# All additions of the experts' outputs on VectorE, and the last choice's outputs loaded over two queues

## The chip, the cores and the metric

The kernel runs on one core of one Trainium2 chip. The metric is the device time of one execution in microseconds (us). A kernel is run several times and the median counts; this kernel before the change has a median of 569.73 us over 3 runs (569.17 to 570.04).

## What is computed

One decoder layer on 1024 tokens of width 256 (16 sequences of 64). It has three parts: self-attention with block-scaled weights, cross-attention with rotary positions, and a mixture of experts. Only the last part matters here:

```
scores = softmax(xt @ Wg.T)                      # 16 experts in 4 groups
topi   = the best 4 experts of the best 2 groups
combine[t, topi] = scores[t, topi]
h = silu(einsum('td,eid->eti', xt, W1)) * einsum('td,eid->eti', xt, W3)
expert_out = einsum('eti,edi->etd', h, W2)
y = einsum('etd,te->td', expert_out, combine)
z = silu(xt @ Ws1.T) * (xt @ Ws3.T) @ Ws2.T      # shared expert
out = x + y + z                                  # x: the residual
```

So each token adds the outputs of four chosen experts ("choices"), each scaled by its score, to the residual.

## The kernel before

The residual `x` is held on chip as eight tiles `x[0]` to `x[7]` of 128 tokens x 256. Experts 0 to 14 are routed: rows of tokens are gathered, sorted by expert, from a buffer `xd` in device memory, an expert works on 384 slots at a time, and its output rows `y` are scattered to a buffer `yd` by three indirect DMAs that GpSimd issues (`send_outputs`, L1296). Expert 15 is the "dense" one: it works on all tokens (`dense_hidden`, `dense_output`), and its result is added to `x` straight from the accumulators, scaled by the token's weight (`add_last`, L944).

In the region of `yd` for choice k lie, for each token, the rows of its k-th choice in the order of the experts. The choices are sorted, so that choice 0 is complete when expert 11 has sent its rows, choice 1 after expert 12, choice 2 after expert 13 and choice 3 after expert 14. `load_outputs(k)` (L1306) then loads the four pieces of choice k, 256 KB each, into tiles `got`; its DMAs are issued by SyncE (L1312), and `behind(got, returned)` makes each of them wait for every scatter sent so far. There are 9 `got` buffers for the 16 pieces, so the later pieces take buffers that earlier additions have read.

`add_outputs(k, got, cw)` (L1319) adds choice k to the eight tiles. For i = 0, 1, 3, 4, 6, 7 VectorE does it in one instruction, `x[i] = y * w + x[i]` (L1326). For i = 2 and 5, ScalarE scales the piece in place (L1323) and GpSimd adds it (L1324). Additions to one tile follow each other in the order of the code.

The last part of the code puts choice 0's additions, the dense expert's output for the first half of the second 512 tokens, choice 1's additions, the dense expert's hidden layer and output for the rest, and choices 2 and 3. The dense expert's hidden layer is a chain over engines: matmuls, SiLU on ScalarE (`g`, L1275 and L1278), the product `h` on VectorE (L1276 and L1279), a rounded copy `hp` on ScalarE (L112), the remainder `hp` on VectorE (L113), and then the matmuls of the output. At the end eight DMAs store `x` (L1384), in turn from SyncE and ScalarE.

The code's order is not the order on an engine. The kernel is built with `schedule_with_timeline_sim=True`: at build time the framework runs the program on a timeline of its own and gives each engine the instruction that is ready there, earlier code first. `tc.issue_after(ins)` adds that an instruction stands behind `ins` on its engine. Once built, each engine works strictly through its list, so a wait holds up what stands behind it, DMA issues on that engine included.

The raw weights of each routed expert are loaded into one of two buffers `w123` of 128 x 1280 (L277) and split into two parts there by ScalarE (L278), VectorE and GpSimd (L283).

Of the kernel before, what the change touches and what calls it, by code (L numbers as in the profile page):

```python
# [25 lines left out]
F32 = mybir.dt.float32  # L26
# [3 lines left out]
AF = mybir.ActivationFunctionType  # L30
ALU = mybir.AluOpType
AX = mybir.AxisListType

B, S, D = 16, 64, 256
NT = B * S
NI = NT // 128
# [6 lines left out]
E, INTER, NGRP, TOPK, TOPKG = 16, 176, 4, 4, 2  # L43
# [4 lines left out]
W_COLS = W_UP + 2 * D  # L48
# [23 lines left out]
def decoder_layer(ctx: ExitStack, tc: tile.TileContext, a: dict, out: bass.AP):  # L72
    nc = tc.nc
# [17 lines left out]
    def av_tile():  # L91
        return ps_av.tile([128, 512], F32, tag="av", name="av")
# [24 lines left out]
    x = [t[:, i, :] for t in x_pairs for i in range(2)]  # L117
# [131 lines left out]
    def behind(read, writes):  # L249
        for w in writes:  # L250
            tc.add_manual_dep(
                read,
                w.name,
                mybir.DependencyInfo(mybir.DependencyClass.Sync, mybir.DependencyReason.DATA),
                reason="it reads rows of each",
            )
# [42 lines left out]
    def expert_output(ps, w, h_p, cols):  # L299


        w2 = [[p[:, W_UP + k * D : W_UP + (k + 1) * D] for p in w] for k in range(2)]
        h = [p[:, cols] for p in h_p]
        return matmuls(
            ps,
            [
                (h[0], w2[0][0]),
                (h[0], w2[0][1]),
                (h[1], w2[0][0]),
                (h[2], w2[1][0]),  # L310
                (h[2], w2[1][1]),
            ],
        )

    with ExitStack() as attn:
# [635 lines left out]
        with (  # L951
# [109 lines left out]
            def dense_weights():  # L1061

                parts = [
                    xw.tile([128, 2, 2, 4 * HQ], F32R, tag=f"w_q{n}", name=f"w_last{n}")
                    .rearrange("p a b c -> p (a b c)")[:, :W_COLS]
                    for n in range(2)
                ]
                up = xb.tile([128, 3, 2, 2, DC], F32, tag="w_s", name="w_last_up")
                down = xb.tile([128, 2, D], F32, tag="w_o0", name="w_last_down")
                for t, cols in (  # L1070
                    (up.rearrange("p a b c d -> p (a b c d)"), slice(0, W_UP)),
                    (down.rearrange("p a b -> p (a b)"), slice(W_UP, W_COLS)),
                ):
                    nc.sync.dma_start(out=t, in_=a["W123"][E - 1][:, cols])
                    parts_of(t, parts[0][:, cols], parts[1][:, cols])
                return parts
# [18 lines left out]
            def dense_gated(g, up, g2, up2):  # L1095
                h_p = [
                    xa.tile([128, 512], F32R, tag=f"roped1{n}", name=f"dense1{n}", bufs=1)
                    for n in range(2)
                ]
                h_p.append(xa.tile([128, 512], F32R, tag="q_r", name="dense2"))  # L1100
                nc.vector.tensor_tensor(g, up, g, ALU.mult)
                parts_of(g, h_p[0], h_p[1])
                nc.vector.tensor_tensor(g2[:64], up2[64:], g2[64:], ALU.mult)
                parts_of(g2[:64], h_p[2][:64], h_p[2][64:])
                return h_p
# [15 lines left out]
            for n in range(len(units) + 2):  # L1121
# [58 lines left out]
                if n == 8:  # L1180
                    w_last = dense_weights()
                    with after(exps[-1]):
                        routed.append(weights_of_choices(0))
                if n == 9:
# [30 lines left out]
                    with after(aimed, placed):  # L1215
# [4 lines left out]
                        h_p = dense_gated(*dense_ups)  # L1220
# [4 lines left out]
    fw = ctx.enter_context(tc.tile_pool(name="fw", bufs=2, reuse_waits="tile"))  # L1225
    fx = ctx.enter_context(tc.tile_pool(name="fx", bufs=2, reuse_waits="tile"))
    fh = ctx.enter_context(tc.tile_pool(name="fh", bufs=2, reuse_waits="tile"))
    fy = ctx.enter_context(tc.tile_pool(name="fy", bufs=2, reuse_waits="tile"))
# [3 lines left out]
    def expert_weights(src, down_lo=nc.gpsimd):  # L1232
        return weight_parts(
            src,
            fw.tile([128, W_COLS], F32, tag="w123", name="w123"),
            [
                fw.tile([128, W_COLS], F32R, tag=f"w123{n}", name=f"w123{n}", bufs=3)
                for n in range(2)
            ],
            down_lo,  # L1240
        )
# [63 lines left out]

    def load_outputs(k):  # L1306

        tiles = []
        for n in range(NI // 2):
            t = fy.tile([128, 2, D], F32, tag="got", name="got", bufs=9)  # L1310
            first = (E - 1) * SLOTS + (TOPK - 1 - k) * NT + n * 256
            got = nc.sync.dma_start(  # L1312
                out=t, in_=yd[first : first + 256].rearrange("(p i) d -> p i d", p=128)
            ).ins
            behind(got, returned)
            tiles.append(t)
        return tiles

    def add_outputs(k, got, cw):  # L1319
        for i in range(NI):  # L1320
            y, w = got[i // 2][:, i % 2], cw[i // 4][:, k, i % 4 : i % 4 + 1]
            if i % 3 == 2:
                nc.scalar.activation(y, y, AF.Copy, scale=w)  # L1323
                nc.gpsimd.tensor_tensor(x[i], x[i], y, ALU.add)  # L1324
            else:
                nc.vector.scalar_tensor_tensor(x[i], y, w, x[i], ALU.mult, ALU.add)  # L1326

    def dense_hidden(w, half, n):
        return expert_hidden(w, [p[:, :, n * 256 : n * 256 + 256] for p in normed[half]], 256)

    def dense_output(w, h_p, half, n, add):
        for b in range(2):
            ps = av_tile()[:, :D]
            expert_output(ps, w, h_p, slice(b * 128, b * 128 + 128))
            add(half, 2 * n + b, ps)
# [6 lines left out]
    ws, xs, hs, got = {}, {}, {}, {}  # L1342
    with tc.issue_after(lows[-1]), tc.issue_after(silus[-1]):
        ws[0] = expert_weights(a["W123"][0], nc.vector)
    for e in range(E + 1):
        if e in (1, 2):

            low = lows[-1]
            hs[e - 1] = expert_hidden(ws[e - 1], xs[e - 1][0], SLOTS)
        if e < E - 1:  # L1350
            low = lows[-1]
            with tc.issue_after(up_done[0] if e in (1, 2) else low):
                xs[e] = expert_inputs(e)
            if e >= 1:
                with tc.issue_after(low), tc.issue_after(silus[-1]):
                    ws[e] = expert_weights(a["W123"][e], nc.vector if e < 3 else nc.gpsimd)
        if e == 1:
            with tc.issue_after(gated[0]), tc.issue_after(silus[-1]):
                routed.append(weights_of_choices(1))
        if 0 <= e - 1 < E - 1 and e > 2:  # L1360
            hs[e - 1] = expert_hidden(ws[e - 1], xs[e - 1][0], SLOTS)
        if e - 2 >= 0:
            if e == E:

                with tc.issue_after(gated[0]):
                    h_p = dense_hidden(w_last, 1, 0)
            last = send_outputs(e - 2, ws.pop(e - 2), hs.pop(e - 2), xs.pop(e - 2)[1])
            if e - 2 == E - TOPK - 2:
                short = slots_are_short()
            k = e - 2 - (E - 1 - TOPK)  # L1370
            if k >= 0:
                got[k] = load_outputs(k)
    with ExitStack() as behind_last:
        for ins in (*last, gated[0]):
            behind_last.enter_context(tc.issue_after(ins))
        cw = [r[0] for r in routed]
        add_outputs(0, got[0], cw)
        dense_output(w_last, h_p, 1, 0, add_last)
        add_outputs(1, got[1], cw)
        dense_output(w_last, dense_hidden(w_last, 1, 1), 1, 1, add_last)  # L1380
        for k in range(2, TOPK):
            add_outputs(k, got[k], cw)
    for i in range(NI):
        (nc.sync if i % 2 == 0 else nc.scalar).dma_start(  # L1384
# [10 lines left out]
    with tc.If(short > 0):  # L1395
        w_over = [weights_without_slot(half, routed[half][2]) for half in range(2)]
        with tc.For_i(0, E - 1, 1) as e:
            w = expert_weights(a["W123"][bass.ds(e, 1)].rearrange("o p c -> p (o c)"))
            for half in range(2):
                dense_expert(w, half, add_over)  # L1400

                t = fs.tile([128, 4, E], F32, tag="slot", name="w_next")
# [110 lines left out]
```

## Time and profile before

| | |
|---|---|
| median of 3 runs | 569.73 us |
| the profiled execution | 570.74 us |
| its span, first to last instruction | 569.0 us |
| TensorE matmul busy | 537.4 us (94%) |
| VectorE busy | 400.9 us (70%) |
| ScalarE busy | 279.3 us (49%) |
| GpSimd busy | 230.5 us (41%) |
| last matmul starts | 559.66 us |
| last VectorE addition starts | about 564.0 us |

In the profile PE is TensorE, DVE is VectorE, ACT is ScalarE, POOL is GpSimd and SP is SyncE; a "q" behind a name marks work of the engine's sequencer, such as the issue of a DMA. Times are us from the start of the span. Instructions of one line that follow each other are merged in the timeline, with their number after an x; what stands in square brackets is the engine's idle time before them and what ended it. Matmuls fill the span up to about 546 us. The change lies wholly behind that, in the last 23 us.

### The profile page before, as it was taken

The page shows a single profiled execution, that of the slowest core. Times are in us where ns is not written, and L with a number is a line of the kernel's source. Part 1 is how long each engine was busy: PE and PEld are TensorE (multiplying, and loading weights), DVE is VectorE, ACT ScalarE, POOL GpSimd, SP SyncE. Part 2 cuts the span into 40 slices and gives each one's busy share as a digit, 9 for nine tenths or more (in the row PEclk, how much of TensorE's full clock was granted, in tenths as well). Part 3 has the DMA queues.
Part 4 walks back from the last instruction along what each step waited for, and adds up shares of the span by engine and source line. Part 5 has one row for each costly group of instructions (what it writes and reads, how often), then busy time and mean ns, then how long its engine had stood idle before and what let it go on. Part 6 is the DMA issues. An engine that isn't in the chain of part 4 may idle for free.

```text
span 569.0 us, 10603 instructions
## 1 busy us (share of the span) xinstructions
PE 537.4 (94%) x4013; PEld 444.5 (78%) x4013; DVE 400.9 (70%) x879; ACT 279.3 (49%) x524; POOL 230.5 (41%) x213
## 2 busy tenths in 40 slices
PE   7999999999999998999999999999999879999961
PEld 6888898988989876667687676676788779999961
DVE  5456555644555788767485686888878678999876
ACT  4677556575565533131323324143445368777551
POOL 4160500102000104434441445453445738888862
PEclk9999999999999999999999999999999989999995
DMA  8654431724300499564010000000322667776374
GB/s 213 163 170 129 129 106 44 205 95 108 97 1 1 119 289 277 140 188 127 2 52 20 8 1 1 0 30 1 105 106 80 209 217 255 244 249 239 123 272 164
DMA packets 44262, 70.83 MB, mean 124 GB/s; under 512 B 11824, under 2 KB 25232, under 8 KB 44208
## 3 DMA queue, kind: packets, MB, share of 16 engines
q1 hardware_dynamic: 39376, 58.71, 34.7%
q0 software_dynamic: 3696, 10.36, 4.7%
q10 hardware_dynamic: 1136, 1.05, 0.6%
q8 instruction: 33, 0.54, 0.4%
q14 instruction: 21, 0.17, 0.1%
HBM read 48.61 MB, written 21.86 MB: 124 GB/s over the span
## 4 chain that ended last, share of the span: by engine, by line
PE 76%; DVE 11%; DMA 4%; issue 3%; ACT 3%; POOL 1%; SPq 0%; DVEq 0%; ACTq 0%; POOLq 0%
PE mm L104 45%; PE mm L997 7%; PE av L582 5%; PE at L565 4%; PE av L104 3%; PE at L343 3%; PE at L1020 2%; PE av L1033 2%; PE mm L431 2%; DMA yd<-y,to 2%; ACT w L278 1%; DMA w<-in_W 1%; DVE hp L113 1%; DVE w L283 1%; DVE x L1326 1%
## 5 line engine op out<-in xcount | busy, mean ns | idle before, releaser
L982 POOL TENSOR_TENSOR roped<-rt,rt 128x512 f32<-128x512 f32 x48 | 62.6, 1326 | 83.3 <-DVE rt L976 80.4
L976 DVE TENSOR_TENSOR rt<-mm,rope_q 128x512 f32<-128x512 f32 x96 | 61.4, 684 | 24.3 <-PE mm L104 23.6
L104 PE MATMUL mm<-xn,w_q 128*128 128x512 f32 x288 | 73.9, 403 | 0.5 <-ACT xn L222 0.5
L104 PEld LDWEIGHTS mm<-xn,w_q 128*128 128x128 f32 x288 | 52.2, 188 | 14.1 <-issue 1.8
L104 PE MATMUL mm<-xs,w 128*128 128x384 f32 x270 | 54.2, 348 | 6.0 <-ACT xs L112 3.0
L1296 POOL DMA_INDIRECT yd<-y,to x45 | 48.7, 1082 | 19.4 <-ACT y L1291 8.0
L104 PEld LDWEIGHTS mm<-xs,w 128*128 128x128 f32 x270 | 47.0, 193 | 8.3 <-ACT xs L112 4.0
L327 ACT ACTIVATE p<-p 128x512 f32<-128x512 f32 x32 | 20.1, 629 | 62.3 <-DVE p L326 62.3
L324 DVE TENSOR_REDUCE sm_m<-at 128x8 f32<-128x512 f32 x32 | 21.8, 680 | 36.1 <-PE at L565 35.2
L997 PE MATMUL mm<-roped,w_s 128*64 128x512 f32 x192 | 46.4, 601 | 0.7 <-POOL roped L982 0.7
L514 POOL TENSOR_TENSOR wv<-code,scale 128x512 fp32r<-128x512 f32 x7 | 9.0, 1282 | 87.4 <-DMA scale<-in_scales 50.3
L605 DVE TENSOR_TENSOR x<-mm,x 128x256 f32<-128x256 f32 x64 | 26.0, 419 | 24.0 <-PE mm L104 22.8
L104 PE MATMUL mm<-wo,o 128*128 128x256 f32 x256 | 39.6, 295 | 0.0
L104 PE MATMUL mm<-xn,wq 128*128 128x512 f32 x128 | 34.6, 404 | 0.7 <-ACT xn L222 0.5
L104 PE MATMUL av<-w,hp 128*128 128x256 f32 x225 | 35.0, 289 | 0.3 <-ACT y L1291 0.3
L104 PE MATMUL mm<-wv,xn 128*128 128x256 f32 x256 | 35.2, 288 | 0.0
L104 PE MATMUL mm<-xn,wk 128*128 128x512 f32 x128 | 34.9, 405 | 0.0
L582 PE MATMUL av<-pt,v 128*128 128x128 f32 x256 | 34.5, 277 | 0.0
L104 PEld LDWEIGHTS mm<-wo,o 128*128 128x128 f32 x256 | 32.9, 190 | 1.5 <-issue 0.4
L582 PEld LDWEIGHTS av<-pt,v 128*128 128x128 f32 x256 | 32.0, 191 | 1.2
L104 PEld LDWEIGHTS mm<-wv,xn 128*128 128x128 f32 x256 | 31.8, 189 | 0.9
L514 POOL TENSOR_TENSOR wo<-code,scale 128x512 fp32r<-128x512 f32 x8 | 10.9, 1368 | 52.0 <-PE mm L104 39.6
(216 smaller groups left out, 1163.8 us busy)
## 6 DMA issues: line engine op xcount, KB each, us to landing
w<-in_W SPq DMA_DIRECT2D x15, 640.0 KB, 4.2
code<-in_codes SPq DMA_DIRECT2D x32, 256.0 KB, 4.4
scale<-in_scales SPq DMA_DIRECT2D x32, 256.0 KB, 4.9
xr<-xd SPq DMA_DIRECT2D x15, 408.0 KB, 4.9
xd<-zeros SPq DMA_DIRECT2D x8, 720.0 KB, 6.8
yd<-zeros SPq DMA_DIRECT2D x8, 512.0 KB, 6.6
got<-yd SPq DMA_DIRECT2D x16, 256.0 KB, 3.6
wq<-in_Wq SPq DMA_DIRECT2D x4, 512.0 KB, 3.7
```

What stands on the lines that cost most here:

```text
L104: m = nc.tensor.matmul(ps, lhsT=l, rhs=r, start=(n == 0), stop=(n == len(pairs) - 1))
L324: nc.vector.tensor_reduce(m, sc, AX.X, ALU.max)
L327: exps.append(nc.scalar.activation(p, p, AF.Exp, scale=scale).ins)
L343: last = nc.tensor.transpose(ps[:, 2 * n : 2 * n + 2, :].rearrange("p a q -> p (a q)"), pn[:, 2 * n : 2 * n + 2, :].rearrange("p a k -> p ...
L514: mults[n] = eng.tensor_tensor(w, *loaded[gr].pop(n), ALU.mult).ins
L565: nc.tensor.matmul(sc[par * 64 : par * 64 + 64, 2 * g + pp, :], lhsT=qk[0][:, b * S : (b + 1) * S], rhs=qk[1][:, b * S : (b + 1) * S], sta ...
L582: nc.tensor.matmul(av[:, k * 128 : (k + 1) * 128], lhsT=v[:, i, k0 : k0 + HD], rhs=pt[:, i].rearrange("p a q -> p (a q)"), start=True, sto ...
L605: nc.vector.tensor_tensor(x[i], ps, x[i], ALU.add)
L976: nc.vector.tensor_tensor(mt, ps3, rope_table(t, 2 * ab + k), ALU.mult)
L982: nc.gpsimd.tensor_tensor(r.rearrange("p (b s) -> p b s", s=S), one, two, op)
L997: nc.tensor.matmul(ps[h // 2][(h % 2) * 64 : (h % 2) * 64 + 64], lhsT=w_s[:, t, blk, ab, :], rhs=roped[2 * t + ab], start=first[h], stop=l ...
L1296: sent = nc.gpsimd.indirect_dma_start(out=yd[: (E - 1) * SLOTS + min(TOPK, E - 1 - e) * NT], out_offset=bass.IndirectOffsetOnAxis(ap=to[:, ...
```

## The change

Three edits. (1) `add_outputs` does all eight tiles on VectorE; the ScalarE scaling and the GpSimd addition for i = 2 and 5 are gone. (2) Choice 3's four pieces go into two tiles of the `w123` tag instead of `got` buffers, and pieces 1 and 3 are issued by ScalarE, 0 and 2 by SyncE as before. (3) In the code, the dense expert's first output stands ahead of choice 0's additions, and choice 1's additions behind all of the dense expert.

```diff
     def load_outputs(k):
 
-        tiles = []
-        for n in range(NI // 2):
-            t = fy.tile([128, 2, D], F32, tag="got", name="got", bufs=9)
+        if k == TOPK - 1:
+            tiles = [
+                t[:, n * 2 * D : (n + 1) * 2 * D].rearrange("p (i d) -> p i d", i=2)
+                for t in (fw.tile([128, W_COLS], F32, tag="w123", name="got_last") for _ in range(2))
+                for n in range(2)
+            ]
+        else:
+            tiles = [
+                fy.tile([128, 2, D], F32, tag="got", name="got", bufs=9) for _ in range(NI // 2)
+            ]
+        for n, t in enumerate(tiles):
             first = (E - 1) * SLOTS + (TOPK - 1 - k) * NT + n * 256
-            got = nc.sync.dma_start(
+            got = (nc.scalar if k == TOPK - 1 and n % 2 else nc.sync).dma_start(
                 out=t, in_=yd[first : first + 256].rearrange("(p i) d -> p i d", p=128)
             ).ins
             behind(got, returned)
-            tiles.append(t)
         return tiles
 
     def add_outputs(k, got, cw):
         for i in range(NI):
             y, w = got[i // 2][:, i % 2], cw[i // 4][:, k, i % 4 : i % 4 + 1]
-            if i % 3 == 2:
-                nc.scalar.activation(y, y, AF.Copy, scale=w)
-                nc.gpsimd.tensor_tensor(x[i], x[i], y, ALU.add)
-            else:
-                nc.vector.scalar_tensor_tensor(x[i], y, w, x[i], ALU.mult, ALU.add)
+            nc.vector.scalar_tensor_tensor(x[i], y, w, x[i], ALU.mult, ALU.add)
...
         cw = [r[0] for r in routed]
+        dense_output(w_last, h_p, 1, 0, add_last)
         add_outputs(0, got[0], cw)
-        dense_output(w_last, h_p, 1, 0, add_last)
-        add_outputs(1, got[1], cw)
         dense_output(w_last, dense_hidden(w_last, 1, 1), 1, 1, add_last)
-        for k in range(2, TOPK):
+        for k in range(1, TOPK):
             add_outputs(k, got[k], cw)
```

## The prediction

> **What bounds the kernel now.** I read the page's slices first: matmuls fill the span to about 546 us, and everything the change touches runs behind that. So I asked for busy time in four stretches of the tail (columns: us, then busy us of PE, PEld, DVE, ACT, POOL with counts, granted clock, DMA share, GB/s):
>
> ```profile
> 545.90:549.60 3.70, 3.44 (x30) 3.24 (x28) 3.66 (x10) 2.53 (x7) 2.79 (x4) 1.00 0.96 368
> 549.60:551.30 1.70, 0.00 (x0) 0.00 (x0) 0.00 (x0) 0.32 (x1) 1.68 (x3) 1.00 0.41 147
> 551.30:564.50 13.20, 3.21 (x10) 2.36 (x10) 12.91 (x23) 2.85 (x6) 5.58 (x7) 0.60 0.67 223
> 564.50:569.00 4.50, 0.00 (x0) 0.00 (x0) 0.00 (x0) 0.00 (x0) 0.00 (x0) 0.50 0.19 64
> ```
>
> VectorE is busy 12.91 of 13.20 us up to the last addition, and before that it stands still for 1.7 us. TensorE has little left. Behind the last addition come 4.5 us of stores and closing semaphores, which the change leaves alone. So the end is VectorE's: the time of its last addition plus 4.5.
>
> The waits of the tail say who holds whom (total, times, longest), then SyncE's own:
>
> ```profile
> PE av L104 <- DVE x L944: 6.4, 2, 4.9
> ACT got L1323 <- DMA got<-yd: 4.5, 5, 2.0
> ACT hp L112 <- DVE h L1276: 3.5, 1, 3.5
> DVE x L1326 <- DMA got<-yd: 1.8, 1, 1.8
> ```
> ```profile
> SPq L1312 <- DMA yd<-y,to: 15.6, 3, 7.0
> ```
>
> TensorE and ScalarE wait for VectorE; VectorE waits once, for a piece of an early choice; SyncE waits 15.6 us for scatters to land. Last, the timeline of VectorE and GpSimd:
>
> ```profile
> 545.93 3.66 DVE L1326 SCALAR_TENSOR_TENSOR x<-got,cw,x 128x256 f32<-128x256 f32 x9
> 550.51 2.09 POOL L1324 TENSOR_TENSOR x<-x,got 128x256 f32<-128x256 f32 x3
> 551.35 1.55 DVE L1326 SCALAR_TENSOR_TENSOR x<-got,cw,x 128x256 f32<-128x256 f32 x1 [1.76 <-DMA got<-yd]
> 552.92 0.42 DVE L1276 TENSOR_TENSOR h<-mm,g 128x256 f32<-128x256 f32 x1
> ...
> 554.63 1.35 DVE L1326 SCALAR_TENSOR_TENSOR x<-got,cw,x 128x256 f32<-128x256 f32 x2
> ...
> 556.58 1.71 POOL L1324 TENSOR_TENSOR x<-x,got 128x256 f32<-128x256 f32 x2 [0.88 <-DVE x L944]
> 556.75 1.82 DVE L1326 SCALAR_TENSOR_TENSOR x<-got,cw,x 128x256 f32<-128x256 f32 x2
> ...
> 559.05 2.63 DVE L1326 SCALAR_TENSOR_TENSOR x<-got,cw,x 128x256 f32<-128x256 f32 x4
> ```
>
> Nine additions take 3.66 us while GpSimd only issues scatters: 0.40 from start to start, 0.48 for one. Beside GpSimd's additions they stretch: 1.55 where 0.48 is due; 1.35 for two where 0.88 is due; 1.82 where 0.88; 2.63 for four where 1.68. Together 1.07 + 0.47 + 0.94 + 0.95 = 3.4 us.
>
> The account closes. VectorE's tail holds 24 additions of choices, 4 of the dense expert (L944) and 4 steps of its hidden layer (h and hp, twice each): 32 x 0.40 = 12.8. Add 3.4 of stretching, 1.76 of waiting and 0.5 of small gaps (the remainder), and from 545.93 one is at 564.4, where the last addition ends.
>
> **The change, part by part.** *Eight additions move to VectorE:* 8 x 0.40 = +3.2 us, all on the path. *GpSimd's additions go:* -3.4, if its additions cause the stretching. A rule could make this void: the Trainium skill's page "GPSIMD Engine Reference", section "8. Key points", says GpSimd shares its SBUF interfaces with VectorE and contends with two-input VectorE instructions, without exempting its DMA issues. Taken that widely, choice 0's eight additions, which run beside the scatters at 546 to 550 us, would pay 8 x 0.47 = 3.8 us, and the gain would be gone. The row of nine at 0.40 apart, beside four scatter issues, says that issues do not stretch additions. I take the row: 0.
>
> *ScalarE's eight scalings go* (0.50 each, 8 x 0.50 = 4.0 us of ScalarE). Now g (L1275) starts at 549.15, behind four of them that waited for pieces; its matmuls began at 545.87 and it could start near 547. So h need not come at 552.92, and hp and the dense output (matmuls at 556.55 and 559.07) come earlier. None of this is on the path by itself, but it gives VectorE work early.
>
> *The wait of 1.76 us* (549.59 to 551.35) is for choice 1's last piece, which lands at 551.25, with h queued behind it. In the new code choice 1 stands behind the dense expert. From 545.93 VectorE has 8 additions of choice 0, two L944 (their matmuls end at 549.34) and the four hidden steps, 14 x 0.40 = 5.6 us, before choice 1 is needed: 551.5, when the piece is there. So -1.76, provided those 14 can flow. What is late next is choice 2: its pieces are issued from 550.83 and land from about 553.4, and VectorE reaches them 8 + 2 instructions later, at 555.5. Choice 3 follows 8 x 0.40 later, at 558.7.
>
> *The second queue.* The last scatter is issued at 549.54 and lands near 552.2. SyncE then is just done with choice 2's issues and issues choice 3's four from 552.74 to 554.56. ScalarE could issue its two from 552.3. The skill's page "DMA: Bandwidth & Descriptors", section "Issuing engines are not separate DMA queues", says that all queues run on the same 16 engines and a second issuer saves only issue time; by it the gain is two issues, 2 x 0.4 = 0.8 us, at the front of the transfers. The trace gives less:
>
> ```profile
> 551.90:558.10 6.20, 1.99 (x6) 1.43 (x6) 6.07 (x11) 1.83 (x4) 3.11 (x5) 0.66 0.95 317
> ```
>
> The DMA engines are 95% busy (third column from the right is the clock, then DMA share) from 551.9 to 558.1; earlier issue only reorders what they carry. I take 0. The price of this edit isn't bandwidth: ScalarE's two issues wait for all scatters, as SyncE's do for 15.6 us, and ScalarE works its list in order. Behind them may stand g, hp's casts (0.41 each) or only the final stores. No row shows ScalarE in such a wait; bounds: 0 if only stores stand behind, and 3.6 us (below) if g does. A gain below nothing is excluded, since the DMA engines are full. I take 0: freed of scalings, g could start near 547 and the casts follow h by about 0.6 (now 552.92 to 553.38), near 549 to 550, well ahead of the landing at 552.2. That the build's own timeline sees it so is the weakest step.
>
> *The buffers.* Sixteen pieces in nine buffers become twelve in nine and four in raw-weight buffers, last read at 538.14 (GpSimd's L283). The waits list shows SyncE held by scatters alone, so this gives nothing; it costs nothing while choice 0 is added before 551, which the 14 instructions cover. *Stores:* eight as before, 0.
>
> Sum: +3.2 - 3.4 - 1.8 = -2.0. Last addition 562.4, span 567.0, profiled execution 570.74 - 2.0 = 568.7. The three runs' median is 1.0 below that execution, so the forecast is 569.73 - 2.0 = **567.7**.
>
> **Rivals.** (a) *The casts stand behind ScalarE's two issues.* For: the landings and the second half's cast are about 2 us apart in my sum, the build's timeline may differ. VectorE reaches the last hp after 13 instructions, at 551.1; ScalarE is free at 552.2 plus semaphores and two issues, 553.2, the cast ends at 553.6: idle 2.5. Sum -2.0 + 2.5 = +0.5, less 0.4 for each choice-1 addition listed ahead of it: 569.4 to 570.2, take **569.8**. Chance 0.30.
>
> (b) *Slower: g itself stands behind them.* Place: ScalarE after its last y copy (546.45). g then ends at 553.6; VectorE has only choice 0 and two L944, 10 x 0.40, to 549.9, then idles 3.6, with 30 instructions left: -2.0 + 3.6 = +1.6, **571.3**. It decides as soon as VectorE's idle time exceeds 2.0 us, and shows beyond 3.1. Against: g's matmuls are done 4 us before the landing. Chance 0.15.
>
> (c) *Pieces rule.* Choice 2 shares the DMA engines with ScalarE's pieces and lands later, or a choice-3 addition stands ahead of choice 2's. Loads now end near 559.3; an addition reached at 557.5 to 558.7 would wait 0.6 to 1.2 us: **568.5**. For: 95% DMA. Against: the total carried is unchanged. Chance 0.13.
>
> My forecast has 0.42. That the edits don't do as they say is only possible for the order, which (a) to (c) cover.
>
> **Numbers.** About 0.2%, 1.1 us, is what a measurement of this kernel can tell from no change. Faster by more: the forecast and most of (c), 0.52. Within: (a) and the rest of (c), 0.33. Slower: (b), 0.15. The range leaves out most of (b) and the forecast's fast edge: 566.9 (no gaps of 0.5, nothing waiting) to 570.8.
>
> **What would show it.** Right: additions all near 0.48 with no GpSimd work behind 551; no VectorE gap before 555 above 0.5; last addition near 562.4. Wrong: a ScalarE gap up to 552 to 553 ended by the scatters' landing, with h or hp behind it on VectorE (a, b); VectorE waiting for got after 555 (c); additions of 0.95 without GpSimd's (the stretching had another cause, then +3 us).

## The result and the profile after

| | median | runs | ratio to before, 95% interval |
|---|---|---|---|
| before | 569.73 us | 5 | |
| after | 571.60 us | 5 | 1.0033 [1.0019, 1.0048] |

The change made the kernel slower by about a third of a per cent, 1.9 us, where 2.0 us less were forecast. The profiled execution of after took 571.04 us, with a span of 569.3 us. The later comparisons ran on five chips, on which before took 569.7, 577.8, 573.2, 572.9 and 577.7 us; on the two slowest single times scattered by some 2%, which makes those intervals wide, and single executions more than 1.5% above the fastest of their kernel are left out of the ratios. So below only ratios to before on the same chip are compared. After gave 1.0023 [1.0009, 1.0036] and 1.0024 [1.0011, 1.0037] on two of them: the loss is real.

The groups of instructions of before and of after, in that order (busy us, mean ns of one | idle before, and what ended it), show the first part of the sum. This is before:

```profile
L1326 DVE SCALAR_TENSOR_TENSOR x<-got,cw,x 128x256 f32<-128x256 f32 x24 | 13.6, 621 | 1.9 <-DMA got<-yd 1.8
L1324 POOL TENSOR_TENSOR x<-x,got 128x256 f32<-128x256 f32 x8 | 6.4, 817 | 4.1 <-ACT got L1323 2.1 <-DMA got<-yd 1.0 <-DVE x L944 0.9
```

And this is after:

```profile
L1329 DVE SCALAR_TENSOR_TENSOR x<-got,cw,x 128x256 f32<-128x256 f32 x24 | 10.3, 479 | 2.5 <-DMA got<-yd 2.4
L1329 DVE SCALAR_TENSOR_TENSOR x<-got_last,cw,x 128x256 f32<-128x256 f32 x8 | 3.5, 477 | 1.0 <-DMA got_last<-yd 1.0
```

The mean addition fell from 621 to 479 ns, so 32 additions keep VectorE busy for 13.8 us where 24 kept it for 13.6. What grew is the last column: idle time before additions that wait for a piece went from 1.8 to 2.4 + 1.0 us.

The timeline of VectorE in the tail of after shows where (start, us, what; the idle time ahead of it in brackets):

```profile
544.71 3.65 DVE L1329 SCALAR_TENSOR_TENSOR x<-got,cw,x 128x256 f32<-128x256 f32 x9
548.39 0.43 DVE L1276 TENSOR_TENSOR h<-mm,g 128x256 f32<-128x256 f32 x1
...
549.70 0.88 DVE L944 SCALAR_TENSOR_TENSOR x<-av,cl,x 128x256 f32<-128x256 f32 x2
552.97 0.88 DVE L1329 SCALAR_TENSOR_TENSOR x<-got,cw,x 128x256 f32<-128x256 f32 x2 [2.39 <-DMA got<-yd]
553.76 0.42 DVE L113 TENSOR_TENSOR hp<-h,hp 128x256 fp32r<-128x256 f32 x1
554.10 1.67 DVE L1329 SCALAR_TENSOR_TENSOR x<-got,cw,x 128x256 f32<-128x256 f32 x4
555.80 0.42 DVE L113 TENSOR_TENSOR hp<-h,hp 64x256 fp32r<-64x256 f32 x1
556.25 0.49 DVE L1329 SCALAR_TENSOR_TENSOR x<-got,cw,x 128x256 f32<-128x256 f32 x1
557.70 1.67 DVE L1329 SCALAR_TENSOR_TENSOR x<-got_last,cw,x 128x256 f32<-128x256 f32 x4 [0.96 <-DMA got_last<-yd]
```

`h` now comes at 548.39 in place of 552.92, as argued. After the two dense additions, 14 instructions behind the start of choice 0's additions, VectorE stands at choice 2's first piece for 2.39 us, with the `hp` step, two additions of choice 0 and half of choice 1 queued behind it. At 556.73 it stands again, for 0.96 us, at choice 3's first piece, in front of three additions of choice 1 and four of choice 2. The order on the engine is not that of the code. (Which choice an addition belongs to is worked out here from the order that the code asks for on each tile; the profile names them all `got`.)

The busy time by stretches (us; busy us of PE, PEld, DVE, ACT, POOL with counts; clock; DMA share; GB/s) splits the tail at the two waits:

```profile
544.70:550.60 5.90, 3.74 (x32) 3.56 (x30) 5.77 (x14) 1.54 (x4) 3.65 (x4) 1.00 0.76 281
550.60:552.97 2.37, 0.53 (x4) 0.30 (x2) 0.00 (x1) 0.38 (x1) 0.00 (x0) 0.96 0.71 218
552.97:556.73 3.76, 1.26 (x4) 0.97 (x5) 3.70 (x9) 0.03 (x1) 0.00 (x0) 0.50 1.00 343
556.73:557.70 0.97, 0.76 (x4) 0.47 (x3) 0.01 (x2) 0.00 (x0) 0.00 (x0) 0.50 0.75 289
557.70:564.51 6.81, 0.00 (x0) 0.00 (x0) 6.81 (x17) 0.00 (x0) 0.00 (x0) 0.50 0.36 121
```

Outside of the two waits VectorE is full. From the start of choice 0's additions to the end of the last one ("the tail" from here on) it is 564.51 - 544.71 = 19.8 us; before it was 564.44 - 545.93 = 18.5. The waits more than account for it: 3.35 in place of 1.76. The starts of the tails (544.71 and 545.93) differ by more than the medians do; the profiles under "Each part alone" below start it anywhere from 543.8 to 545.3 us. So one profile tells where VectorE stands, and the repeated timings tell what that is worth.

### The profile page after: what moved, and what is told of

It reads as the page before. It is cut to its first block, busy times and chain, and to the rows that moved or that the text cites. A ratio compares the mean times of both kernels' runs of the same rounds, so it can differ in the third digit from the quotient of the medians.

```text
span 569.3 us, 10588 instructions
## 1 busy us (share of the span) xinstructions
PE 536.3 (94%) x4013; PEld 443.8 (78%) x4013; DVE 401.1 (70%) x887; ACT 275.7 (48%) x516; POOL 224.8 (39%) x205
## 4 chain that ended last, share of the span: by engine, by line
PE 79%; DVE 10%; ACT 4%; DMA 2%; issue 2%; POOL 1%; SPq 0%; DVEq 0%; ACTq 0%; POOLq 0%
PE mm L104 47%; PE mm L997 7%; PE av L582 5%; PE at L565 4%; PE av L104 4%; PE at L343 3%; PE at L1020 2%; PE av L1033 2%; PE mm L431 2%; ACT w L278 2%; DMA yd<-y,to 1%; DVE w L283 1%; PE mm L453 1%; DVE hp L113 1%; DMA got_last<-yd 1%
## 5 line engine op out<-in xcount | busy, mean ns | idle before, releaser
L327 ACT ACTIVATE p<-p 128x512 f32<-128x512 f32 x32 | 20.1, 629 | 62.3 <-DVE p L326 62.3
L104 PEld LDWEIGHTS av<-w,hp 128*128 128x128 f32 x225 | 30.9, 193 | 1.2 <-ACT y L1291 0.6
```

Of the source, the lines that this page charges most:

```text
L104: m = nc.tensor.matmul(ps, lhsT=l, rhs=r, start=(n == 0), stop=(n == len(pairs) - 1))
L327: exps.append(nc.scalar.activation(p, p, AF.Exp, scale=scale).ins)
```

## The experiments

Three theories were held. Theory 1: VectorE's built list puts additions in front of ready work although their pieces have not landed. Theory 2: ScalarE's two issues, which wait for the scatters, hold its last `hp` cast and what needs it. Theory 3: choice 3's two pieces on a second queue take transfer time from the pieces on SyncE's queue that VectorE needs first.

### Each part alone

The first three kernels are before with one part of the change each; the fourth is after without the second queue.

```diff
 # e1_vector_only: before, with
-            if i % 3 == 2:
...
+            nc.vector.scalar_tensor_tensor(x[i], y, w, x[i], ALU.mult, ALU.add)
 # e2_queue_only: before, with the change's load_outputs
 # e3_order_only: before, with the change's order of the last part
 # e4_after_sync: after, with
-            got = (nc.scalar if k == TOPK - 1 and n % 2 else nc.sync).dma_start(
+            got = nc.sync.dma_start(
```

> The kernel before with the first edit alone (all eight tiles' additions on VectorE; loads and code order as before). Theory 1 (VectorE's work is as summed, but its list holds additions whose pieces have not landed in front of work that is ready): VectorE's list, as built, has choice 2's first four additions in front of both hp steps, and choice 3's first four in front of choice 2's last four. From the start of choice 0's additions (T0), 18 instructions of 0.40 us bring it to T0+7.2, the first piece of choice 2 lands at T0+7.5 to 8.2; later it waits again for choice 3's first piece (T0+12.1 to 13.0). Stalls of 0.3 to 1.0 and 1.0 to 1.4 us, last addition at T0+17.7 to 18.6, against 18.5 before and 19.8 in the changed kernel: 569.0 to 569.8 us, no change to 0.1% faster. Theory 2 (ScalarE's two issues in front of the hp cast are the cause of the loss): without them the whole forecast gain shows, 567.7 us.

> The kernel before with the second edit alone (choice 3's pieces in the raw weights' buffers, two of them issued by ScalarE). VectorE's list as built is that of the kernel before, ScalarE's has the two issues between the two hp casts. Theory 1: the second cast is needed on VectorE only 4 us after the scatters land, so the issues hold up nothing: 569.2 to 570.2 us, no change. Theory 2: the cast and with it the dense expert's output come later, about 1 to 2 us slower, 570.7 to 571.7.

> The kernel before with the third edit alone (the code's order of dense output and choice 1; additions shared by three engines and loads as before). Theory 1: in VectorE's list as built choice 2's first addition stands behind only 14 instructions (T0+5.6, against T0+7.5 to 8.2 for its piece), so a stall of about 2 us takes the place of the 1.76 us one, and choice 3's first addition stands in front of 9 others. Last addition T0+18 to 19: 569.3 to 570.5 us, no change to slightly slower. Theory 2: no ScalarE issue is there, so nothing is lost, and the earlier dense output gains up to 1 us: 568.7 to 569.7.

> The changed kernel with all four of choice 3's loads issued by SyncE (still into the raw weights' buffers). Theory 1: VectorE's list still has choice 2's first two additions behind 14 instructions and in front of hp, and choice 3's first four in front of ten others: stalls of about 2 and 1 us, last addition T0+18.9 to 19.8, 570.5 to 571.5 us, within 1 us of the changed kernel. Theory 2: the hp cast is free of the issues, the loss goes away: 567.5 to 569 us.

| on the same chip, before 569.73 us (67 runs) | ratio | tail in its profile | waits for pieces there |
|---|---|---|---|
| all additions on VectorE | 0.9997 [0.9990, 1.0005] | 17.4 us | 0.44 + 0.34 |
| second queue alone | 1.0009 [1.0002, 1.0017] | 18.7 | 2.11 + 0.71 |
| order alone | 0.9989 [0.9981, 0.9996] | 18.6 | 1.56 |
| after, loads by SyncE | 0.9995 [0.9984, 1.0006] | 20.1 | 3.75 |

No part alone loses more than 0.1%; only the second queue's interval lies above 1 (0.09%, 0.5 us). Together the three parts would give -0.05%, so the loss of after would come from how they work on each other. The last row is the telling one: without ScalarE's two loads the loss is gone, although its profiled execution has the longest wait of all for choice 2's first piece:

```profile
549.98 0.88 DVE L944 SCALAR_TENSOR_TENSOR x<-av,cl,x 128x256 f32<-128x256 f32 x2
554.61 0.88 DVE L1329 SCALAR_TENSOR_TENSOR x<-got,cw,x 128x256 f32<-128x256 f32 x2 [3.75 <-DMA got<-yd]
...
556.70 1.67 DVE L1329 SCALAR_TENSOR_TENSOR x<-got,cw,x 128x256 f32<-128x256 f32 x4
558.29 1.66 DVE L1329 SCALAR_TENSOR_TENSOR x<-got_last,cw,x 128x256 f32<-128x256 f32 x4
```

There is no second wait here, at choice 3's first piece. Theory 1 had expected 570.5 to 571.5 us of this kernel, and its median was 569.42: theory 1 is not the loss. Theory 2 missed too, with 567.5 to 569. Of the other forecasts, theory 1's came true for the first two kernels (medians 569.28 and 570.14) and theory 2's for the third (568.95). One caution: without ScalarE's issues the build also gave VectorE a slightly different list (one addition, not four, between the two `hp` steps), so this kernel does not differ from after by the queue alone. The length of the wait for choice 2 is not fixed by the kernel either: SyncE issued choice 2's first piece 4.7 to 6.4 us behind the start of the tail in these four profiles, since the scatters that it waits for landed at different times, and this same kernel waited only 0.64 us for it in the profile of a later run.

### A forced order

The first of these kernels is after with choice 2's additions behind choice 1's last one on VectorE and choice 3's behind choice 2's. Two more begin the order earlier, behind the last gated product (the last `hp` step): one with the loads of the change, one with all loads by SyncE. After itself was timed beside them.

```diff
-            nc.vector.scalar_tensor_tensor(x[i], y, w, x[i], ALU.mult, ALU.add)
+            last_add = nc.vector.scalar_tensor_tensor(x[i], y, w, x[i], ALU.mult, ALU.add).ins
+        return last_add
 # g1a_order_casts_behind and b3_chain_scalar_loads
-        for k in range(1, TOPK):
-            add_outputs(k, got[k], cw)
+        last_add = add_outputs(1, got[1], cw)
+        for k in range(2, TOPK):
+            with tc.issue_after(last_add), tc.issue_after(gated[0]):
+                last_add = add_outputs(k, got[k], cw)
 # g1b_order_casts_first; with all loads by nc.sync g2b_order_sync and b4_chain_sync_loads
+        last_add = gated[0]
         for k in range(1, TOPK):
-            add_outputs(k, got[k], cw)
+            with tc.issue_after(last_add):
+                last_add = add_outputs(k, got[k], cw)
```

> The changed kernel once more, beside the next three and the kernel before on one chip. Theory 1 and 2 alike: as before, 0.2 to 0.5% slower than the kernel before, 570.8 to 572 us. If it is not slower here, the first result was partly chance.

> The changed kernel with VectorE's list put in the order in which pieces land: choice 2's additions behind choice 1's last and behind the last hp step, choice 3's behind choice 2's last. ScalarE's two issues still stand in front of its last hp cast. Theory 1 (list order): the wait for choice 2's and 3's pieces goes, but now the last hp step is in front of everything: its cast comes at T0+8 to 9 (scatters land at about T0+6.3, then two issues), and the dense expert's output 1.3 us later, so VectorE idles some 2 to 3 us once; last addition T0+17.9 to 18.9, 569.2 to 570.1 us. Theory 2 (the issues hold the casts, and that was the whole loss): no change from the changed kernel, 571 us. Theory 3 (two queues: ScalarE's pieces take DMA time from choice 2's and from choice 3's first piece): those pieces are no longer waited for, so a gain of about 1 us against the changed kernel, 570.5.

> As the run before, with choice 1's additions too behind the last hp step, and so built that both hp casts stand in front of ScalarE's two issues. Theory 1: 13 instructions to hp at T0+5.2, choice 1 and the dense output to T0+9.6, choice 2 to T0+12.8, choice 3 to T0+16.0 to 16.6, with no wait over 0.5 us: 567.3 to 567.8 us. Theory 2: the same. Theory 3: the pieces of choices 2 and 3 land no later than T0+13, in time: the same. It shows whether the sum of the prediction holds once nothing is waited for; if it stays at 569 or above, the sum itself was wrong.

> The same VectorE list as the run before, all loads issued by SyncE. Theory 1 and 2: the same time as the run before within 0.3 us, 567.3 to 567.8. Theory 3: up to 0.5 us faster or slower, as pieces come in another order but are waited for by nobody.

The ratios were 1.0016 [0.9987, 1.0045] for after, 1.0010 [0.9987, 1.0033], 1.0004 [0.9976, 1.0032] and 0.9996 [0.9973, 1.0020]: too wide to tell these kernels apart. The profiles did what the order was to do: no wait for a piece in any of the three forced ones, and tails of 17.2, 17.8 and 16.4 us. Four kernels were then timed side by side on another chip:

> The kernel after, unchanged, side by side with the three others of this call. Theory 1 (VectorE's built list puts additions whose pieces have not landed in front of ready work) and theory 3 (ScalarE's two loads delay what VectorE waits for) both expect 1.002 to 1.004 times the kernel before, and in the profile two waits for pieces on VectorE of 1.7 to 3.5 us together, with the last addition 18.5 to 20 us behind the start of choice 0's. If the loss of 0.33% was only the few runs it was measured with, the ratio is 0.999 to 1.001.

> The kernel after with all four pieces of choice 3 loaded by SyncE (the same kernel as the earlier run of that edit). Theory 1: the order of the additions is nearly the same, the waits stay, so 1.002 to 1.004, as the kernel after. Theory 3, and theory 2 (ScalarE's issues hold its last cast): the loss is in the two issues on ScalarE, so 0.999 to 1.0005, and 0.2 to 0.4% under the kernel after of this call.

> The kernel after with choice 2's additions put behind choice 1's on VectorE and choice 3's behind choice 2's; the loads as in the kernel after, on two queues. Theory 1: the waits for pieces vanish, the last addition ends 17.0 to 17.5 us behind the start of choice 0's in place of 18.5 to 19.8, so 1.3 to 2.5 us, 0.2 to 0.45%, under the kernel after of this call: 0.998 to 1.000 of before. Theory 3: the order is not what costs, and the time stays within 0.1% of the kernel after.

> The same order, begun behind the last gated product, with choices 1 to 3 each behind the one ahead, and all loads by SyncE. Theory 1: VectorE has no wait left behind its 27 additions, the last one ends 16.4 to 17.0 us behind the start of choice 0's, some 1.5 us ahead of the kernel before's 18.5: 0.996 to 0.998 of before, and 0.4 to 0.6% under the kernel after. Rival: the end is not set by VectorE's tail alone (the start of choice 0's additions comes later by what the tail saves, or the stores set the end), and the ratio stays at 0.999 to 1.001.

| before 573.24 us (67 runs) | ratio | tail in its profile |
|---|---|---|
| after | 1.0023 [1.0009, 1.0036] | 21.9 us |
| after, loads by SyncE | 0.9994 [0.9982, 1.0007] | 19.1 |
| forced order, the change's loads | 1.0022 [1.0011, 1.0033] | 18.2 |
| forced order begun earlier, loads by SyncE | 1.0016 [1.0005, 1.0027] | 19.3 |

The first two rows confirm it: the loss comes and goes with ScalarE's two loads. The third speaks against theory 1 as the whole cause: its profile has no wait for a piece, and the time is after's. It is not a clean test, though, since other waits stand in that profile:

```profile
556.15 0.43 DVE L1276 TENSOR_TENSOR h<-mm,g 128x256 f32<-128x256 f32 x1 [1.10 <-ACT g L1275]
...
561.59 0.91 DVE L944 SCALAR_TENSOR_TENSOR x<-av,cl,x 128x256 f32<-128x256 f32 x2 [0.89 <-PE av L104]
```

The fourth kernel met neither its forecast (0.996 to 0.998) nor that of its rival (0.999 to 1.001): it is slower than before with no load on the second queue at all. The timeline of VectorE in after on this chip has both waits for pieces, and a new one ahead of them:

```profile
548.96 3.66 DVE L1329 SCALAR_TENSOR_TENSOR x<-got,cw,x 128x256 f32<-128x256 f32 x9
554.57 0.42 DVE L1276 TENSOR_TENSOR h<-mm,g 128x256 f32<-128x256 f32 x1 [1.95 <-remote]
...
558.00 0.88 DVE L1329 SCALAR_TENSOR_TENSOR x<-got,cw,x 128x256 f32<-128x256 f32 x2 [1.25 <-DMA got<-yd]
...
564.03 1.67 DVE L1329 SCALAR_TENSOR_TENSOR x<-got_last,cw,x 128x256 f32<-128x256 f32 x4 [2.27 <-DMA got_last<-yd]
```

"Remote" means that the trace names nothing that ended the wait; the step needs TensorE's hidden products and ScalarE's `g`. The same wait is 1.93 us in the kernel with SyncE's loads. Where only six additions are listed ahead of it, as in the fourth kernel, it is the longest wait of the tail, the likely reason for that kernel's loss, since nothing in it waited for a piece (not shown: on the previous chip the same kernel waited only 0.19 us there):

```profile
548.63 2.46 DVE L1329 SCALAR_TENSOR_TENSOR x<-got,cw,x 128x256 f32<-128x256 f32 x6
554.18 0.42 DVE L1276 TENSOR_TENSOR h<-mm,g 128x256 f32<-128x256 f32 x1 [3.08 <-remote]
```

### The issues without their transfers, and the transfers without ScalarE

The first of these kernels is the control that the question needs: all four pieces by SyncE, and ScalarE issues two loads of 8 KB at the places of its two of 256 KB, with the same waits. The lists of VectorE and ScalarE are the same as those of after, instruction for instruction; only what the second queue carries differs. The third puts eleven additions ahead of the last hidden step, and choices 2 and 3 in order behind choice 1.

```diff
 # c1_tiny_issues: all pieces by nc.sync, and
+            if k == TOPK - 1 and n % 2:
+                probe = fy.tile([128, 16], F32, tag="probe", name="probe", bufs=2)
+                behind(nc.scalar.dma_start(out=probe, in_=yd[first : first + 128, :16]).ins, returned)
 # c2_gpsimd_issues
-            got = (nc.scalar if k == TOPK - 1 and n % 2 else nc.sync).dma_start(
+            got = (nc.gpsimd if k == TOPK - 1 and n % 2 else nc.sync).dma_start(
 # c3_chain_all_first and d1_chain_again: before, with all additions by nc.vector, and
-        add_outputs(1, got[1], cw)
+        last_add = add_outputs(1, got[1], cw)
         dense_output(w_last, dense_hidden(w_last, 1, 1), 1, 1, add_last)
         for k in range(2, TOPK):
-            add_outputs(k, got[k], cw)
+            with tc.issue_after(last_add), tc.issue_after(gated[0]):
+                last_add = add_outputs(k, got[k], cw)
```

> All four pieces of choice 3 by SyncE, and in place of ScalarE's two loads two loads of 128x16 numbers into a tile that nothing reads, at the same places and with the same waits; the lists of VectorE and ScalarE are those of the kernel after, instruction for instruction. Theory 2 (the issues hold ScalarE's last cast and with it the list): 1.002 to 1.0035, as the kernel after. Theory 3 (the transfers of the second queue delay choice 3's first piece on the first): the loss is gone, 0.999 to 1.0005, and VectorE's wait for choice 3's first piece falls from about 1 to 2.3 us to under 0.7 us.

> The kernel after with choice 3's second and fourth piece issued by GpSimd, behind its last scatters, in place of ScalarE: nothing of VectorE's or ScalarE's stands behind these issues, the transfers still go by another queue than SyncE's. Theory 2: no cast is held, so 0.999 to 1.0005. Theory 3: the second queue still takes half of the transfer time from SyncE's pieces, so 1.0015 to 1.0035, with a wait of 1 us or more for choice 3's first piece.

> All additions by VectorE, all loads by SyncE into the buffers of before, choice 0's and 1's additions at their places of before, choice 2's behind choice 1's last one and the last gated product, choice 3's behind choice 2's: eleven additions stand ahead of the last dense products, and none ahead of its piece. Theory 1: no wait for a piece, the last addition 16.5 to 17.4 us behind the start of choice 0's, 0.996 to 0.999 of before. Rival: as with the chain that begins earlier (1.0016), what VectorE saves on pieces it waits elsewhere, 1.000 to 1.002.

> The kernel after, unchanged, as the anchor of this call. All theories: 1.002 to 1.0035 of before; the comparison of the other three with it is what counts.

| before 572.87 us (52 runs) | ratio | tail in its profile | wait for choice 3's first piece |
|---|---|---|---|
| tiny loads by ScalarE | 0.9999 [0.9982, 1.0016] | 18.7 us | none |
| two loads by GpSimd | 1.0008 [0.9990, 1.0025] | 18.1 | none |
| eleven ahead, then in order | 0.9981 [0.9964, 0.9997] | 17.4 | none |
| after | 1.0024 [1.0011, 1.0037] | 19.2 | 0.95 |

The loads by GpSimd come out between the two theories and settle nothing: GpSimd issued its pieces only behind SyncE's two (at 557.28 and 557.87 us, against 556.56 and 556.97), and VectorE's list is another one. The tiny loads speak against theory 2. VectorE's waits, first of this kernel, then of after beside it (total, times, longest):

```profile
DVE h L1276 <- remote: 1.9, 1, 1.9
DVE x L1332 <- DMA got<-yd: 0.3, 1, 0.3
```
```profile
DVE h L1276 <- remote: 2.0, 1, 2.0
DVE x L1329 <- DMA got_last<-yd: 1.0, 1, 1.0
```

And ScalarE's two issues and the cast behind them, in the same order of the kernels:

```profile
554.80 0.87 ACTq L1326 DMA_DIRECT2D probe<-yd  x2
555.72 0.41 ACT L112 CAST hp<-h 64x256 fp32r<-64x256 f32 x1 [1.63 <-DVE x L944]
```
```profile
555.98 0.84 ACTq L1320 DMA_DIRECT2D got_last<-yd  x2
556.87 0.41 ACT L112 CAST hp<-h 64x256 fp32r<-64x256 f32 x1 [1.61 <-DVE x L944]
```

The cast stands behind the issues in both, with the same idle time of 1.6 us ahead of it. With the hold and the very same lists, but without the transfers, the time is that of before. The ratio intervals of this kernel and of after overlap by 0.05%, but the two can be compared directly: the single times of after are longer by 1.1 us in the mean (95% interval 0.3 to 1.9, if the executions are independent). Against the kernel with SyncE's loads, on the previous chip, they are longer by 1.7 us (1.0 to 2.4). So the hold costs nothing that can be seen, and what costs is the half megabyte of choice 3 on a second queue.

The chain of work that ended last runs over choice 3's first piece in both profiles. It gives the piece's issue by SyncE and the time to its landing, first with tiny loads, then in after:

```profile
554.95 4.52 DMA got_last<-yd
```
```profile
555.88 5.29 DMA got_last<-yd
```

The other traces say the same. Where SyncE issued this piece within 0.8 us of choice 2's last one, it took 5.45 us in the first profile of after, 6.76 us in the one with the tail of 21.9 us and 6.24 us with the second queue alone, but 4.6 us in after with SyncE's loads, 4.7 us with the order alone and 5.2 us in before.

What the second queue does is seen in the DMA view of the first profile of after, from 552 to 558 us (queue, packets, MB, share of the 16 engines; then the issues with the median us to landing): SyncE's queue, q1, and ScalarE's, q10, are served side by side, and together keep the engines busy for 93% of the time.

```profile
q1 hardware_dynamic: 804, 1.45, 68.9%
q10 hardware_dynamic: 288, 0.52, 23.9%
...
got_last<-yd ACTq DMA_DIRECT2D x2, 256.0 KB, 4.6
got_last<-yd SPq DMA_DIRECT2D x2, 256.0 KB, 5.5
got<-yd SPq DMA_DIRECT2D x1, 256.0 KB, 5.3
```

ScalarE's first piece, issued at 551.70, lands at 556.3, ahead of choice 2's last piece, which SyncE issued at 551.66 and which lands at 557.0, and of choice 3's first, at 557.67, for which VectorE waits. In before the pieces whose landing the trace tells land in the order of the choices.

### The faster order again, and the trace of before beside it

> The same kernel as the earlier run with all of choice 0's and the first of choice 1's additions ahead of the last dense products. If its gain is real: 0.997 to 0.999 of before, and a last addition 16.5 to 17.5 us behind the start of choice 0's. If it was chance: 0.9995 to 1.001.

> The kernel before, unchanged, for its trace. In its list twelve steps stand ahead of the last dense hidden products' step on VectorE, some of them stretched by GpSimd to 0.9 us, so it comes there 6 to 7 us behind the start of choice 0's additions. If TensorE's signals come late here too, at 5.5 us, VectorE does not wait for them in this kernel, where the kernel after waits 2 us; the last addition ends 18 to 19 us behind the start of choice 0's.

The order with eleven ahead gave 0.9979 [0.9956, 1.0002] against a before of 577.70 us (27 runs), after 0.9981 [0.9964, 0.9997]: two estimates of about -0.2%, of which one interval lies wholly below 1. The timeline of its first profile shows the eleven additions ahead of `h`, and the wait there down to 1.13 us:

```profile
547.33 4.44 DVE L1322 SCALAR_TENSOR_TENSOR x<-got,cw,x 128x256 f32<-128x256 f32 x11
552.90 0.42 DVE L1276 TENSOR_TENSOR h<-mm,g 128x256 f32<-128x256 f32 x1 [1.13 <-remote]
```

In the second profile the tail was 16.3 us; neither has a wait for a piece. Besides "order alone" (0.9989) this is the only kernel of the study with an interval that lies below 1, and it also beats after. In before's trace on that chip VectorE stood 1.87 us at choice 1's last piece, as in the first profile, and did not wait at `h`, which comes 7.0 us behind the start of the tail; the tail was 18.4 us.

## Why the prediction was wrong

Two terms of the sum failed: the -1.8 for the wait, of which 0.3 us or less came, and the 0 for the second queue, which cost 1.0 to 1.7 us and so made the change a loss. The +3.2 and the -3.4 held.

*Additions and stretching: right.* +3.2 - 3.4 was the sum; busy time of the additions went from 13.6 to 13.8 us, each takes 0.48 with GpSimd silent, and choice 0's additions beside the scatters' issues stay at 0.40 from start to start (nine in 3.65 us).

*The wait of 1.76 us: the first step that failed.* The wait for choice 1's last piece is gone, and 14 instructions do stand ahead of the next one, but that the number fits is luck: the prediction counted eight additions of choice 0 and four hidden steps among them, and the build put six of choice 0, four of choice 1 and two hidden steps there. "VectorE reaches them 8 + 2 instructions later, at 555.5" failed: choice 2's first two additions come right behind those 14, since the build placed them there, and wait 2.39 us. The rule that the framework takes what is ready on its own timeline was known; the step assumed the code's order all the same. With an order that has ready work in front, 1.1 to 1.2 us of the 2.0 appeared (0.9981 and 0.9979). That order also keeps the loads off the second queue, so it is not the change with one repair; the nearest order with the change's own loads, nine ahead, gave 1.0022.

*The second queue: the second step that failed.* "Earlier issue only reorders what they carry. I take 0", and "a gain below nothing is excluded". The lower bound was right and the upper bound looked at the wrong thing: it priced the hold on ScalarE, up to 3.6 us, and not the reordering. On the chips where both were timed side by side, after stands 0.29% above itself with SyncE's loads (1.0023 against 0.9994) and 0.25% above itself with tiny loads (1.0024 against 0.9999): 1.4 to 1.7 us that should have stood in the sum (the plain medians differ by 1.3 and 1.0 us). On the shared engines the Trainium skill's page "DMA: Bandwidth & Descriptors", section "Issuing engines are not separate DMA queues", and the trace agree (68.9% and 23.9% of the same 16 above). The section says as well that such transfers interleave, but the only effect that it puts a price on is issue time, and the prediction took it so. With the engines full, what comes early for a late addition makes another piece late for an early one.

*"The weakest step", the casts behind ScalarE's issues: true, and harmless.* The last cast did stand behind the issues in the first profile of after, and ScalarE was idle for 3.3 us ahead of it:

```profile
551.70 0.85 ACTq L1320 DMA_DIRECT2D got_last<-yd  x2
552.59 0.40 ACT L112 CAST hp<-h 64x256 fp32r<-64x256 f32 x1 [3.33 <-issue]
```

VectorE, which stood at a piece until 552.97 and had seven instructions to do first, took it up at 555.80, 2.8 us after it was done at 552.99. The rival on it named a real wait and the wrong price. The slower rival, `g` behind the issues at 571.3, came near the measured 571.6 by number only: `g` started at 545.65, six microseconds ahead of the issues. The pieces' rival (chance 0.13) had the mechanism, choice 2 landing later by ScalarE's pieces and a choice-3 addition listed too early; its 0.6 to 1.2 us were too small against the 3.35 us of waits for pieces, and it stood beside the forecast's full gain. Nothing rests on one small misreading: of the four scalings ahead of `g` in before, two waited for pieces (0.80 and 0.17 us), not all four.

*The account.* The forecast was -2.0. Kernels with the change's additions and order but SyncE's loads are at 0.9994 and 0.9995, -0.3 us, and the one with tiny loads at 0.9999: 1.7 to 2.0 us of the gain did not come, and the second queue adds 1.0 to 1.7. Together this gives +0.7 to +1.7. After shows 1.3 and 1.4 us on the two chips where it was timed beside them; the first timing showed 1.9, with 1.1 to 2.7 as its interval.

*What stays open.* That the transfers on the second queue cost is shown; that they do it by the wait for choice 3's first piece is supported by the waits of three profiles of after (0.96, 2.27, 0.95 us; at most 0.34 in the kernels with SyncE's loads) and by the landing times above, but the forced order with the change's loads has no such wait in its profile and still takes 1.0022. There 1.10 us were spent at `h` and 0.89 at the dense additions, and whether the second queue has a hand in these no run told. Nor was it settled why "order alone" gains 0.1% with a tail as long as before's. Of the 1.7 us that did not come, the waits for choice 2 and for `h` are the likely places, not shown to be the sum.

## What to carry to other kernels

Here the DMA engines were 93% busy, and moving two of four pieces to a second queue made a piece that was needed early land later, 5.3 us after its issue in place of 4.5. So where transfers fill the engines, ask who arrives first, and put the pieces in the order of their use, on one queue if need be. When additions move to one engine, read what the build puts on that engine's list before counting a removed wait as gained: here 1.76 us of one wait became 3.35 us of two others. And where an engine's list is the bound, the steps that others produce late (here `h`) want ready work in front of them: on the two chips with the longest waits there, VectorE stood at `h` for 3.08 us with six additions ahead of it, for 1.1 to 2.0 us with nine and for 1.13 us with eleven.

## What the runs showed of the hardware that was not expected

In most profiles from the four slower chips TensorE's completion signals of the tail (the steps of the semaphore by which it tells that matmuls are done) came bunched. In the profile of after with the tail of 21.9 us four of them came within 0.2 us, 5.5 us behind the start of the tail; in after's first profile they came singly between 0.9 and 3.5 us, with records of matmuls that look the same. In all eight profiles from the two chips with before at 573.24 and 572.87 us VectorE waited 1.1 to 3.1 us at `h`. On the last chip the bunch came at 1.6 to 1.9 us, in before as well, and neither kernel waited there. These traces also lack some of the signals, so the cause is not told.

Landing times of the scatters moved by 1.7 us between executions on one chip (SyncE's first load of choice 2 at 4.7 to 6.4 us into the tail), as much as the whole effect under study. The kernels of these profiles differ in the order of the tail, and whether that has a part in it is open.
